# Iterated square roots of 1024 matrices, then a filtered Fourier layer: nine sets in flight instead of seven, and shorter rounds

## The chip, the cores and the metric

The kernel runs on one core of a Trainium2 chip. The metric is the device time of one execution in microseconds. Of the kernel before, three executions are shown: 3199.45, 3210.22 and 3218.83 us, median 3210.22. The profile is of one more execution, which took 3217.96 us.

[...] PE multiplies matrices into PSUM, DVE (VectorE) and ACT (ScalarE) read the results from there, POOL (GpSimd) adds what lies in SBUF, and SP issues most of the transfers; ACT issues those of the input.

## The reference, cut to what matters

`x` is 32 images of 32 channels of 128 x 128 float32. Two layers add to it:

```python
# layer 0, for each image and channel; gn normalizes groups of 2 channels
A = gn(x)
Y, Z = A / norm(A), I
for _ in range(5):
    T = 0.5 * (3.0 * I - Z @ Y)
    Y, Z = Y @ T, T @ Z
x = x + Y * sqrt(norm(A))
# layer 1
f = fft2(gn(x)).real
g = zeros; g[:32, :32] = einsum(f[:32, :32], weights1); g[-32:, :32] = einsum(f[-32:, :32], weights2)
x = x + ifft2(g).real
```

Layer 0 is 1024 independent chains of 128 x 128 products; layer 1 mixes the channels of an image, mode by mode.

## The kernel before, in words

**Sets.** Four channels of an image make a set; there are 256 sets, eight to an image. A set is a Python generator, `newton`, which yields after each step; the five iterations are folded there into two polynomials of fourth degree (`quartic`, called twice) and a last product. A step is nearly always: four products of 128 x 128 on PE into one bank of PSUM (`products`, L298, or `transposed`, L304), and one instruction of DVE (`plus`, L273) or ACT (`taken`, L267) that takes them out to SBUF. The next step needs that result. The chain of one set is v, w, q, then y, m, mb, again v, w, q, then t and y4, t, and the addition to xt at L410.

**Far and near.** w is a transposed v plus r. Images 1 to 19 (`is_far`) get it with transfers: DVE transposes blocks of 32 x 32 (L360), SP stores the tile in DRAM (L362), a later step loads it again with its blocks exchanged (one transfer at L373, or four at L370 in the second `quartic`), and POOL adds r (L376). The other images get it with a transposition on PE. So an image of the first kind makes fewer products, and needs more transfers.

**Rounds.** The loop at the end steps through lanes: each of the `LANES` lanes holds one set, and each round takes every lane one yield further. A new set enters a free lane when `due` allows: one per `FAR` rounds for a far image (20/7, since `newton` takes 20 steps and there are 7 lanes), one per `NEAR` rounds for a near one (13/4), which also needs fewer than `LESS` lanes taken. As a set enters, the normalization of the next is queued (`staged`), and the input of a later one is fetched (`fetch`, on ACT's queue). The tile scheduler then orders the instructions by the order of the program, their dependencies and its own estimate of when each is ready; instructions within `kept` stay in program order on their engine.

**Other generators** are stepped in the same loop: `prep` (statistics of the next image, from tiles `xs` loaded on ACT's queue, L193), `settle` (stores xt into `mid` at L418, folds it on POOL at L423, takes statistics at L427), `forward` and `spectrum` (the forward transform), `wide_products` and `small_products` (channel mixing, for a group of 21, then 8, then 3 images), and `inverse` (back transform, L742 to L781). Only after all sets of a group are there can its mixing begin, so inverses run beside the sets of the images from 20 on, and those of the last images after the last set.

**Buffers.** `rooms` gives, for each kind of tile, how many buffers of 128 x 512 float32 there are for the whole run, and how many more in the pool `early`, which is closed after the far images (`change`); `four` takes turns between the two. `far` decides there whether the second are used.

## Time and profile before

| | |
|---|---|
| profiled execution | 3217.96 us |
| its span | 3216.0 us |
| granted clock of TensorE, mean | 0.971 |
| PE busy | 2973.3 us (92%) |
| DVE busy | 2365.3 us (74%) |
| ACT busy | 1716.3 us (53%) |
| POOL busy | 2008.4 us (62%) |
| moved by DMA | 637.55 MB, mean 198 GB/s |

The page lists busy time by engine, by 40 slices of the span, and by line, each line with the idle time of its engine just before it and what ended that. A queue's name with a q (SPq) is the time of its sequencer, which issues transfers. In lists of waits, the line before the arrow waited for what stands after it; the numbers are microseconds in all, how often, and the longest. Four stages can be told apart: far images until about 1720 us, a passage until 1890, near images with mixing and inverses until about 2990, and the end.

### The profile page before, as it was taken

Reading aid. Unit: us, or ns where it says so; the run is one execution under the profiler, and the core shown is the slowest. Engines: PE = TensorE matmul, PEld = TensorE weight load, DVE = VectorE, ACT = ScalarE, POOL = GpSimd, SP = SyncE. Lnnn points to the kernel's source line nnn. Section 1 sums busy time; section 2 is a strip of 40 time slices with the busy share of each in tenths; the row PEclk is TensorE's granted clock in tenths of the full one; section 3 lists DMA queues with packets and bytes.
Section 4 is the critical chain, followed back from the end, with each engine's and each line's share of the span. In section 5 each row is a group of like instructions: output and inputs, shape, how many; then the busy total and the mean of one; then the engine's idle time right before and its main releaser. Section 6 shows DMA issues by size and latency. Waiting matters only on the chain.

```text
span 3216.0 us, 78946 instructions
## 1 busy us (share of the span) xinstructions
PE 2973.3 (92%) x29440; PEld 2836.6 (88%) x29440; DVE 2365.3 (74%) x5672; ACT 1716.3 (53%) x4148; POOL 2008.4 (62%) x2312
## 2 busy tenths in 40 slices
PE   6999999999999999999999999999999998999954
PEld 6889899899999999999999998898889888999853
DVE  5787788778888887888788665577767776756645
ACT  3555555565556655565565555455555544546533
POOL 3566666666767666666676553466767767746642
PEclk9999999999999999999999999999999999999975
DMA  3466566666666666666666336765767676576667
GB/s 122 148 190 190 192 201 202 186 199 204 196 208 200 210 191 196 207 204 200 191 211 193 96 96 207 227 214 185 232 201 243 213 240 208 193 225 209 207 238 255
DMA packets 482317, 637.55 MB, mean 198 GB/s; under 512 B 97936, under 2 KB 263056, under 8 KB 481936
## 3 DMA queue, kind: packets, MB, share of 16 engines
q1 hardware_dynamic: 366448, 413.30, 40.3%
q10 hardware_dynamic: 113472, 211.86, 21.1%
q0 software_dynamic: 2016, 7.34, 0.6%
q8 instruction: 235, 3.85, 0.5%
q14 instruction: 146, 1.20, 0.1%
HBM read 398.75 MB, written 233.57 MB: 197 GB/s over the span
## 4 chain that ended last, share of the span: by engine, by line
PE 67%; DVE 13%; DMA 12%; ACT 3%; issue 2%; POOL 1%; SPq 1%; ACTq 0%; DVEq 0%; POOLq 0%
PE ps L298 55%; PE ps L304 6%; DMA xs<-in_xt 5%; DMA turn<-turn 2%; PE ps L764 1%; DMA w<-turn 1%; DVE a_st L193 1%; PE ps L442 1%; DVE turn L360 1%; DVE q L273 1%; DVE yt L781 1%; DVE v L273 1%; PE ps L576 1%; PE ps L742 1%; DVE xt L410 1%
## 5 line engine op out<-in xcount | busy, mean ns | idle before, releaser
L298 PE MATMUL ps<-w,v 128*128 128x128 f32 x4096 | 548.5, 278 | 26.4 <-POOL w L376 14.1
L376 POOL TENSOR_TENSOR w<-w,r 128x512 f32<-128x512 f32 x304 | 386.7, 1275 | 270.5 <-DMA w<-turn 222.0
L298 PE MATMUL ps<-y,q 128*128 128x128 f32 x4096 | 549.6, 278 | 3.9 <-ACT y L267 2.2
L423 POOL TENSOR_TENSOR fold<-xt 128x256 f32<-128x256 f32 x512 | 363.7, 731 | 279.2 <-DVE xt L410 262.5
L328 ACT ACTIVATE b<-b,a_off,a_scr 128x128 f32<-128x128 f32 x1024 | 463.9, 489 | 129.7 <-issue 54.8
L298 PEld LDWEIGHTS ps<-w,v 128*128 128x128 f32 x4096 | 500.5, 193 | 35.2 <-POOL w L376 20.1
L298 PEld LDWEIGHTS ps<-y,q 128*128 128x128 f32 x4096 | 504.7, 194 | 7.0 <-ACT y L267 3.3
L273 DVE SCALAR_TENSOR_TENSOR q<-ps,eye 128x512 f32<-128x512 f32 x512 | 347.0, 678 | 99.5 <-PE ps L298 97.9
L717 POOL TENSOR_TENSOR yt<-yt,d 128x512 f32<-128x512 f32 x236 | 297.9, 1289 | 188.0 <-ACT d L776 155.0
L193 DVE BATCH_NORM_STATS2 a_st<-xs 128x6 f32<-128x128 f32 x1024 | 231.8, 279 | 143.4 <-DMA xs<-in_xt 143.0
L335 POOL TENSOR_SCALAR x<-xt,a_nm,a_sc 128x128 f32<-128x128 f32 x720 | 317.8, 454 | 23.9 <-DVE a_n L222 20.8
L404 ACT ACTIVATE y<-ps,a_t_s 128x128 f32<-128x128 f32 x1024 | 292.1, 369 | 62.3 <-PE ps L298 61.5
L292 POOL TENSOR_TENSOR r<-b,eye 128x512 f32<-128x512 f32 x104 | 132.8, 1277 | 283.8 <-issue 224.6
L298 PE MATMUL ps<-m,q 128*128 128x128 f32 x2048 | 280.3, 280 | 27.9 <-DVE q L273 27.6
L298 PE MATMUL ps<-m,mb 128*128 128x128 f32 x2048 | 282.4, 282 | 19.6 <-ACT mb L267 19.6
L273 DVE SCALAR_TENSOR_TENSOR v<-ps,x 128x512 f32<-128x512 f32 x256 | 175.5, 686 | 165.0 <-PE ps L298 162.9
L273 DVE SCALAR_TENSOR_TENSOR v<-ps,m 128x512 f32<-128x512 f32 x256 | 174.7, 683 | 162.8 <-PE ps L298 162.1
L298 PE MATMUL ps<-y,t 128*128 128x128 f32 x2048 | 280.6, 281 | 6.6 <-DVE t L273 4.5
L298 PEld LDWEIGHTS ps<-m,q 128*128 128x128 f32 x2048 | 252.1, 194 | 35.4 <-DVE q L273 17.9
L360 DVE STREAM_TRANSPOSE turn<-v 128x512 f32<-128x512 f32 x304 | 277.9, 914 | 7.2
L298 PE MATMUL ps<-x,b 128*128 128x128 f32 x2048 | 275.6, 278 | 5.6 <-POOL x L335 5.6
L298 PEld LDWEIGHTS ps<-m,mb 128*128 128x128 f32 x2048 | 254.9, 196 | 27.7 <-ACT mb L267 25.0
(124 smaller groups left out, 5867.6 us busy)
## 6 DMA issues: line engine op xcount, KB each, us to landing
turn<-turn SPq DMA_DIRECT2D x304, 256.0 KB
b<-in_x ACTq DMA_DIRECT2D x256, 256.0 KB
xt<-in_xt ACTq DMA_DIRECT2D x256, 256.0 KB
xs<-in_xt ACTq DMA_DIRECT2D x256, 256.0 KB
mid<-xt SPq DMA_DIRECT2D x256, 256.0 KB
yt<-mid SPq DMA_DIRECT2D x128, 512.0 KB
out<-yt SPq DMA_DIRECT2D x108, 512.0 KB
w<-turn SPq DMA_DIRECT2D x152, 256.0 KB
```

The source lines that it names most:

```text
L193: nc.vector.bn_stats(st[:, 4 * i + c, :], tiles[i][:, c, :])
L273: nc.vector.scalar_tensor_tensor(s, ps, f, t, ALU.mult, ALU.add)
L292: nc.gpsimd.tensor_tensor(r, mb, eye, ALU.add)
L298: nc.tensor.matmul(ps[:, j, :], lhsT[:, j], rhs[:, j], start=True, stop=True)
L304: nc.tensor.transpose(ps[:, j, :], t[:, j, :], ident)
L328: nc.scalar.activation(t, x, AF.Identity, bias=offset[:, c], scale=scale[:, c])
L335: nc.gpsimd.tensor_scalar(m[:, j, :], xt[:, j, :], nm[:, c // 2 : c // 2 + 1], sc[:, c : c + 1], ALU.add, ALU.mult,)
L360: nc.vector.transpose(blocks(t), v.rearrange(form, b=4))
L376: nc.gpsimd.tensor_tensor(w, w, r, ALU.add)
L404: nc.scalar.mul(y[:, j, :], py[:, j, :], sn[:, c : c + 1])
L423: nc.gpsimd.tensor_tensor(f[:, :, 64 * half : 64 * half + 64], xt[:, :, 0:64], xt[:, :, 64:128], op)
L717: engine.tensor_tensor(yh, yh, d, op)
```

## The change

- **Lanes and rounds.** `LANES, LESS` become 9 and 5, `FAR, NEAR` 27/9 and 25/5. Each step of a set yields twice (`rest`), but for the last. A far set takes 28 rounds instead of 20, a near one 24 instead of 13. The extra yields that only far sets had at q and t are gone. In far sets, one yield lay between store and load of a factor, and two between load and addition; now it is two and two, and the rounds are shorter in the near stage. A set's entry counts a far lane as 0.6 of a near one.
- **Buffers.** `rooms` is dealt anew, and whether a tile may lie in `early` is decided by `has_more`, which holds for the first 166 sets. `xs` has four buffers.
- **Statistics of a group.** `settle` takes the statistics of two channels, which are one group, in one instruction (L427): two of 256 elements for four of 128. `moments`, `avg_0` and `b_st` follow; the values computed are the same.
- **Other generators.** `step` goes on to the next generator of a queue when one is done. Mixing is stepped in two of three rounds, not in each; inverses in one of three, and in the round after the first half of a block (`holding`), where before it was four of five, or each one at the end.

```diff
-LANES, LESS = 7, 4
-FAR, NEAR = 20 / 7, 13 / 4
+LANES, LESS = 9, 5
+FAR, NEAR = 27 / 9, 25 / 5
...
+MORE = FIRST * 8 + 6
...
-    nc.vector.memset(avg_0, -P * P / 512)
+    nc.vector.memset(avg_0, -P * P / 256)
...
-    stp = ctx.enter_context(tc.tile_pool(name="stp", bufs=3))
+    stp = ctx.enter_context(tc.tile_pool(name="stp", bufs=4))
...
-        f = st.rearrange("p (g c) (e t) -> p g (c e) t", c=2, t=3)
+        per = st.shape[1] // G
+        f = st.rearrange("p (g c) (e t) -> p g (c e) t", c=per, t=3)
...
-        nc.vector.tensor_copy(nm, pm)
-        d = small.tile([P, G, 4], F32, tag=f"{tag}_d", name=f"{tag}_d")
+        nc.vector.tensor_scalar_mul(nm, pm, 2 / per)
+        d = small.tile([P, G, 2 * per], F32, tag=f"{tag}_d", name=f"{tag}_d")
...
-    rooms = dict(b=(6, 2), xt=(10, 5), x=(4, 3), r=(4, 3), v=(3, 3), w=(3, 3), q=(3, 3), y=(4, 3))
-    rooms.update(m=(3, 3), mb=(2, 1), t=(3, 2), y4=(2, 2), turn=(0, 3))
+    rooms = dict(b=(4, 2), xt=(10, 4), x=(3, 2), r=(5, 2), v=(3, 3), w=(3, 2), q=(4, 2), y=(4, 2))
+    rooms.update(m=(4, 2), mb=(2, 1), t=(3, 2), y4=(2, 2), turn=(0, 4))
...
+    def has_more(b, g):
+
+        return b * (C // 4) + g < MORE
...
             kept(nc.sync.dma_start(out=held, in_=t.rearrange("p c x -> p (c x)")))
-            yield
-            w = four("w", far)
+            yield from rest
+            w = four("w", more)
...
-            yield
-            yield
+            yield from rest
             nc.gpsimd.tensor_tensor(w, w, r, ALU.add)
             w = blocks(w).rearrange("p a c j -> p c a j")
         else:
-            yield
-            w = plus(transposed(v), 1.0, r, "w", far)
-        yield
-        q = plus(products(v, w), 1 / (16 * QS * QS), eye, "q", far)
-        yield
-        if far:
-            yield
+            yield from rest
+            w = plus(transposed(v), 1.0, r, "w", more)
+        yield from rest
+        q = plus(products(v, w), 1 / (16 * QS * QS), eye, "q", more)
+        yield from rest
         return q
 
-    def newton(g, sn, xt, m, mb, r, far):
+    rest = (None, None)
+
+    def newton(g, sn, xt, m, mb, r, far, more):
...
-        m = taken(products(q, y), "m", far, MS)
-        yield
-        mb = taken(transposed(m), "mb", far, QR * QS / MS)
-        r = plus_eye(mb, far)
-        yield
+        m = taken(products(q, y), "m", more, MS)
+        yield from rest
+        mb = taken(transposed(m), "mb", more, QR * QS / MS)
+        r = plus_eye(mb, far, more)
+        yield from rest
...
-        for j in range(4):
-            nc.vector.bn_stats(st[:, 4 * g + j, :], xt[:, j, :])
+        for j in range(2):
+            nc.vector.bn_stats(
+                st[:, 2 * g + j, :], xt[:, 2 * j : 2 * j + 2, :].rearrange("p c h -> p (c h)")
+            )
...
                 if not i:
+                    holding.append(b)
                     yield
+                    holding.pop()
...
-        if queue and next(queue[0], queue) is queue:
+        while queue and next(queue[0], queue) is queue:
             queue.pop(0)
...
-            room = lanes[i] is None and (far or LANES - lanes.count(None) < LESS)
-            if todo and room and rounds >= due:
+            under_way = [is_far(lane[0]) for lane in lanes if lane]
+            room = far or under_way.count(False) + 0.6 * under_way.count(True) < LESS
+            if lanes[i] is None and todo and room and rounds >= due:
...
-            if i == 0 or tail:
+            if i == 0 and rounds % 3 or tail:
                 step(prods)
-            if i == 0 and (rounds % 5 or len(ended) > B - 6) or tail and not (posts or specs):
+            if i == 0 and (rounds % 3 == 0 or holding) or tail and not (posts or specs):
                 step(backs)
```

## The prediction

> **What bounds the kernel now.** I read the busy shares of the page, then the same by stage (the far stage, the passage to the next, the near stage, the end), then PE's waits, a stretch of its timeline, and SP's queue.

> ```profile
> PE 2973.3 (92%) x29440; PEld 2836.6 (88%) x29440; DVE 2365.3 (74%) x5672; ACT 1716.3 (53%) x4148; POOL 2008.4 (62%) x2312
> ...
> 60.00:1720.00 1660.00, 1588.86 (x14047) 1531.84 (x14048) 1336.02 (x3209) 960.72 (x2368) 1105.20 (x1220) 0.99 0.63 195
> 1720.00:1890.00 170.00, 168.57 (x1523) 162.64 (x1522) 119.70 (x331) 87.36 (x208) 101.11 (x135) 1.00 0.38 120
> 1890.00:2990.00 1100.00, 1044.15 (x11438) 985.70 (x11437) 754.61 (x1803) 564.77 (x1345) 680.64 (x816) 0.99 0.65 211
> 2990.00:3216.00 226.00, 140.09 (x2234) 127.53 (x2233) 122.22 (x215) 87.57 (x193) 101.32 (x105) 0.75 0.72 236
> ```

> The columns are stretch, length, busy us of PE, PEld, DVE, ACT and POOL, clock, DMA share, GB/s. PE sets the time until 2990 us and is idle for 1660 - 1589 = 71 us in the far stage, 1.4 us in the passage and 1100 - 1044 = 56 us in the near stage. Busy time hides a little more. The densest pieces of the chain show the floor:

> ```profile
> 599.87 9.83 PE ps L298 x88
> ```

> 88 PE instructions in 9.83 us are 0.1117 us each; I call that a slot. A product of four matrices is eight slots, 0.89 us. The far stage's 14047 instructions at that rate take 1569 us, so 91 us of its 1660 are excess: the 71 idle, and 20 at a lower clock or in short hiccups. The passage runs at 170/1523 = 0.1116 us: with nothing late, this code reaches the floor. So the most that can be won before 2990 us is about 91 + 56 + 11 (1% of clock in the near stage) = 158 us.

> Which waits make the idle time? PE's own, in the far stage (first four lines) and in the near stage (three lines):

> ```profile
> PE ps L298 <- ACT mb L267: 19.6, 21, 3.4
> PE ps L298 <- POOL w L376: 14.1, 17, 2.1
> PE ps L304 <- ACT m L267: 11.5, 8, 4.2
> ...
> PE ps L298 <- ACT t L267: 3.0, 2, 2.3
> ...
> PE ps L298 <- DVE q L273: 22.3, 16, 6.0
> PE ps L304 <- DVE v L273: 8.7, 3, 6.4
> PE ps L298 <- DVE w L273: 8.6, 7, 2.9
> ```

> (total us, times, longest.) Four kinds make 48 of the 71 us, three make 40 of the 56. All are steps of one set that follow each other too closely on PE. The timeline shows one:

> ```profile
> 1001.94 0.63 PE L304 MATMUL ps<-ident,m 128*128 128x128 f32 x4
> 1003.32 1.16 PE L298 MATMUL ps<-m,mb 128*128 128x128 f32 x8 [0.75 <-ACT mb L267]
> ```

> The product that needs mb is the next thing on PE after the transposition that yields it; ACT's copy (598 ns in its row) lies open between them. SP's queue shows the same of the loads of factors:

> ```profile
> SPq L373 <- DMA turn<-turn: 198.1, 104, 5.4
> SPq L370 <- DMA turn<-turn: 175.9, 105, 4.2
> ```

> 209 loads stood at the head of SP until the store that they read back had landed, 1.8 us each; stores behind them waited too, and so did POOL (222.0 us in 125 waits for w<-turn).

> [...] products recorded at 1.06 us each start 0.89 us apart, so I use starts. [...] Here the longest waits are 3.4 to 6.4 us and the clock is 0.99 in both long stages, so at most 1% lies there. [...] DVE stood at statistics L193 for DMA xs (143.0 us, longest 7.3) while evacuations lay behind. [...]

> **The change part by part.** Its work on PE is the same, 29440 instructions. What changes is the order. I counted, in the order of PE's instructions in the two built programs, how many slots lie between a product and the one that needs its result (medians), and turned them into time with 0.1117 us.

> *Nine lanes, two rounds a step, far stage.* A round stays about as long: 20/7 = 2.86 rounds a set become 28 rounds over 9 lanes = 3.11. A step was one round, now two. Distances: y,q to transposition of m 18 to 48 slots (2.0 to 5.4 us); that to m,mb 24 to 56 (2.7 to 6.3; some were 0); t 32 to 52 (3.6 to 5.8). The gain of 2.2 to 3.6 us exceeds nearly every wait there (longest 3.4, 4.2, 2.3; means 0.9, 1.4, 1.5). Of 19.6 + 11.5 + 3.0 = 34.1 us I count 90% as gone: 31. The distance before y<-q hardly moves (48 to 56 for x,q, the same for m,q), but it costs only 2.6 us there: 0.

> *Loads of factors.* The load (one DMA, or four of 64 KB; 152 + 608 in all) goes from 24 to 48 slots after its store, 2.7 to 5.4 us, past at most one more store on SP. That covers SP's 1.8 us, so it is issued without standing; the addition on POOL stays 22 slots behind it, and the product that uses w goes from 52 to 74 slots behind that. Store to use: 120 to 172 slots, 13.4 to 19.2 us. POOL's wait for the DMA was 1.8 us on average: it mostly goes, and PE's 14.1 us with it. I take 12. Behind POOL's addition stand r, x and fold, which come earlier then.

> Clock in the far stage: 1% of 1660 is 17 us; with fewer pauses half returns, 8. Far stage in all: 31 + 12 + 8 = 51 us. The other 23 us of idle time (statistics L204, L504 and such) keep their distances: 0.

> *Five near lanes of 24 rounds, one set per 5 rounds.* Distances: v to its transposition 24 to 50 slots, w 32 to 46, q 28 to 44: 1.6 to 2.9 us more. Mean waits were 2.9, 1.2 and 1.4, but the longest 6.4, and these come from DVE standing at xs, which stays. I take 60% of 22.3 + 8.7 + 8.6 + 3.9 (m, mb and t) = 26 us, and half of the clock's 11: 5. Near stage 31 us.

> *Statistics over two channels.* 512 calls of 256 elements for 1024 of 128. A call occupies DVE for 236.5/1024 = 0.231 us; per element, the 512-wide sums against the 128-wide call give (0.68 - 0.28)/384 = 1.05 ns, so a wide call is about 0.365 us. 1024 x 0.231 - 512 x 0.365 = 50 us less DVE work, all hidden: DVE is busy 80% in the far stage and 69% in the near, behind PE. On the path 0; between 0 and 10 if DVE's queue matters. Without cover it would be the 50.

> *Pools.* Seventy-seven tiles of four matrices instead of 83, for more sets. I looked how long each buffer stands free, from its last reader to its next writer, in the built order: xt at least 112 slots (12.5 us; it was 286), v 70, w 86, y 72, x 64 in the far stage, b 67 in the near one; x in the near stage down to 0, but is filled long before use. Cost 0, and the slower rival below if a landing outlasts the gap. The fourth xs buffer moves the load from 24 to 30 slots ahead of its statistics in the far stage and not at all in the near (30, 29): 0.

> *Pace of products and inverses.* Two rounds of three and one of three (with the second half of an inverse right after its first). In order, inverse 0 starts 176 slots earlier, inverse 27 38 earlier, and what follows the last set is the same, inverses 28 to 31. The end costs the same 226 us. The short hold of PSUM banks could help PE's weight loads that waited for ACT d (18.3 us in the near stage); peak use of banks is unchanged, so 0, up to 10.

> *Sum.* 51 + 31 = 82 us. The profiled execution took 3217.96 us, its span 3216.0: 3134 of span, 3136. The median of the runs shown, 3210.22, lies 8 us below the profiled one: **3128 us**, 2.6% faster.

> **Rivals.**
> 1. *More comes back.* Half-clock stretches, banks and hiccups follow the pauses: 75 of 91 us far, 50 of 67 near, 3085. For it: the passage at 0.1116 us; against: statistics L204 and xs are untouched. Chance 0.14.
> 2. *The waits move.* DVE's standing at xs, up to 7.3 us, is longer than the new 5 to 6 us, and the q distances stay short; only POOL's and ACT's far waits shrink by half, 22 us: about 3190, between 3165 and 3225. For it: 72 of the 143 us of xs fall in the near stage. Chance 0.16.
> 3. *Slower: ACT stands at a fetch.* xt is fetched on ACT's queue; its 14 buffers serve nine lanes, those staged and those settling. If the store into mid lands later than 12.5 us after the last reader's place, ACT blocks with all its copies behind. ACT idles (1660 - 961)/154 sets = 4.5 us a set; beyond that each us counts. At 5.2 us late: 154 x 0.7 = 108, far gain gone, near 31 kept, + 77: 3287. Against it: SP loses its standing at loads. Chance 0.12.

> **How the numbers follow.** Forecast 0.58, its own range 3100 to 3165. A change below 0.5% (16 us) can't be told from none. Faster: 0.58 + 0.14 + half of rival 2 = 0.80; the same 0.07; slower 0.12 + 0.01 = 0.13. Range 3080 to 3212: it leaves out rival 3 and the tips of 1 and 2.

> **What would show it.** PE's far waits for mb, m and w below 10 us together; SP's standing at L373 and L370's loads below 100 us; POOL's wait for w<-turn below 100; near waits for q, v, w near 16; stage times of about 1609 and 1069 us; wide statistics near 0.41 us each. Wrong would be: ACT waiting for DMA mid<-xt ahead of xt (rival 3), or PE's waits for q and v as large as before with xs ahead on DVE (rival 2).

## The result: 0.24% faster, a tenth of what was forecast

The changed kernel took 3199.91 us (median of 20 runs, 3189.05 to 3210.8), the one before 3207.38 (20 runs): a ratio of 0.9976, with a 95% interval of 0.9964 to 0.9989. Forecast were 3128 us, range 3080 to 3212, against 3210 before: a gain of 82 us. It was 7.5. The result lies inside the range, which was wide enough for the rivals, but outside the 3100 to 3165 us that the forecast gave itself. The profiled execution has a span of 3205.1 us against 3216.0.

The page and the windows of the changed kernel, with the same columns as before:

```profile
PE 2973.7 (93%) x29440; PEld 2850.6 (89%) x29440; DVE 2316.5 (72%) x5158; ACT 1701.5 (53%) x4148; POOL 2003.6 (63%) x2314
```

```profile
60.00:1720.00 1660.00, 1605.95 (x14232) 1558.02 (x14232) 1304.12 (x2935) 970.36 (x2396) 1117.20 (x1243) 0.98 0.64 198
...
1890.00:2990.00 1100.00, 1033.77 (x11303) 978.40 (x11302) 740.32 (x1618) 546.80 (x1324) 680.32 (x817) 0.98 0.65 213
```

In the far stage PE idles 54 us instead of 71, but its clock fell from 0.99 to 0.98; in the near stage it idles 66 instead of 56, and the clock fell as much. PE's waits show what took the place of the old ones, first in the far stage. Source lines have moved by two or more: L206 is the former L204, L509 the former L504, L300 the former L298, L447 the former L442.

```profile
PE ps L206 <- DVE a_qs L201: 16.0, 9, 2.6
PE ps L509 <- DVE b_qr L504: 8.1, 4, 2.7
PE ps L206 <- DVE b_r_q L150: 7.1, 2, 3.7
PE ps L206 <- DVE b_inv L521: 5.2, 2, 3.2
PE ps L206 <- DVE b_r_q L152: 4.4, 2, 2.5
PE ps L300 <- POOL w L381: 3.6, 2, 2.2
PE ps L306 <- ACT sw L464: 2.7, 8, 0.5
```

And in the near stage:

```profile
PE ps L206 <- DVE a_qs L201: 17.9, 6, 8.9
PE ps L447 <- POOL fold L426: 12.0, 6, 4.4
PE ps L300 <- ACT d L782: 11.3, 4, 4.5
PE ps L509 <- DVE b_qr L504: 6.7, 3, 3.1
```

The far waits for mb and t, 22.6 us together before, are gone from the list; that for m is 1.0 us, that for w 3.6 instead of 14.1. In the near stage q, v and w cost 39.6 us before and do not stand among the first now. In their place come two tiny products: L206, which averages an image's statistics across the partitions (two instructions of 32 columns), and L509, which does so for a spectrum. L206 reads only a_qs of what DVE makes; where the list names b_r_q or b_inv there, another instruction of DVE ended nearest to the release. Before, the wait for a_qs was short, in the far stage (first line) and in the near one:

```profile
PE ps L204 <- DVE a_qs L199: 6.9, 6, 2.1
...
PE ps L204 <- DVE a_qs L199: 3.2, 4, 1.1
```

One such place of the changed kernel on PE's timeline:

```profile
885.63 0.22 PE L512 MATMUL ps<-avg,b_mr 128*32 128x1 f32 x2
889.23 0.60 PE L206 MATMUL ps<-a_qs,avg_mean 128*128 128x32 f32 x2 [3.38 <-DVE b_r_q L150]
889.64 2.05 PE L300 MATMUL ps<-x,q 128*128 128x128 f32 x8
891.49 0.85 PE L300 MATMUL ps<-q,t 128*128 128x128 f32 x3
```

PE stands 3.4 us at L206 with ready products behind it. DVE meanwhile works through the chain that leads to a_qs, in which other instructions lie:

```profile
887.26 0.67 DVE L174 TENSOR_TENSOR a_d<-a_d 128x64 f32<-128x64 f32 x1
887.85 0.14 DVE L516 TENSOR_SCALAR b_v<-ps 128x1 f32<-128x1 f32 x1
887.92 0.14 DVE L517 COPY b_v<-ps 32x1 f32<-32x1 f32 x1
887.98 0.64 DVE L175 SCALAR_TENSOR_TENSOR a_d<-a_d,a_st 128x64 f32<-128x64 f32 x1
888.55 0.41 DVE L430 BATCH_NORM_STATS2 b_st<-xt 128x6 f32<-128x256 f32 x1
888.88 0.20 DVE L201 TENSOR_REDUCE a_qs<-a_d 128x32 f32<-128x64 f32 x1
```

And the next eight instructions of PE take 2.05 us instead of 1.06; the clock that the trace records is 0.50 from 887.74 to 894.57 us. Such stretches, recorded at 0.5, are called half clock here. Of the 14 in the far stage, 13 begin within 2 us of the end of a pause at L206 or L509. A pause, here and below, is the time between two starts on PE less one slot, and is counted where it exceeds 0.35 us. By stages, which end at the additions to xt that end images 0, 19 and 31 (all in us):

| | start | far | near | end | pauses far, near | half clock far, near |
|---|---|---|---|---|---|---|
| before | 135.4 | 1648.2 | 1309.4 | 123.1 | 80.9, 75.3 | 37.5, 41.0 |
| changed | 143.8 | 1631.2 | 1306.3 | 123.8 | 56.0, 83.1 | 58.0, 61.4 |

### The profile page after: what moved, and what is told of

Its sections match the earlier page's. It is cut to its first block, busy times and chain, and to the rows that moved or that the text cites. A ratio compares the mean times of both kernels' runs of the same rounds, so it can differ in the third digit from the quotient of the medians.

```text
span 3205.1 us, 78907 instructions
## 1 busy us (share of the span) xinstructions
PE 2973.7 (93%) x29440; PEld 2850.6 (89%) x29440; DVE 2316.5 (72%) x5158; ACT 1701.5 (53%) x4148; POOL 2003.6 (63%) x2314
## 4 chain that ended last, share of the span: by engine, by line
PE 68%; DVE 12%; DMA 11%; issue 3%; POOL 3%; ACT 2%; SPq 1%; ACTq 0%; DVEq 0%; POOLq 0%
PE ps L300 55%; PE ps L306 6%; DMA xs<-in_xt 4%; DMA w<-turn 2%; DVE turn L366 2%; PE ps L770 2%; PE ps L447 1%; DVE v L275 1%; DVE a_st L195 1%; POOL yt L723 1%; DVE q L275 1%; DMA yt<-mid 1%; PE ps L748 1%; DVE yt L787 1%; PE ps L581 1%
## 5 line engine op out<-in xcount | busy, mean ns | idle before, releaser
L300 PE MATMUL ps<-w,v 128*128 128x128 f32 x4096 | 556.2, 280 | 8.9 <-POOL w L381 3.6
L300 PE MATMUL ps<-y,q 128*128 128x128 f32 x4096 | 531.2, 278 | 11.8 <-ACT d L782 9.9
L300 PEld LDWEIGHTS ps<-w,v 128*128 128x128 f32 x4096 | 506.2, 195 | 13.3 <-POOL w L381 5.8
L300 PEld LDWEIGHTS ps<-y,q 128*128 128x128 f32 x4096 | 496.6, 195 | 16.0 <-ACT d L782 10.4
L195 DVE BATCH_NORM_STATS2 a_st<-xs 128x6 f32<-128x128 f32 x1024 | 227.2, 279 | 134.3 <-DMA xs<-in_xt 133.7
L294 POOL TENSOR_TENSOR r<-mb,eye 128x512 f32<-128x512 f32 x104 | 132.5, 1274 | 304.4 <-ACT mb L269 298.9
L300 PE MATMUL ps<-x,b 128*128 128x128 f32 x2048 | 279.4, 280 | 5.7 <-POOL x L341 5.6
L269 ACT ACTIVATE t<-ps 128x512 f32<-128x512 f32 x256 | 152.5, 596 | 247.6 <-PE ps L300 240.6
L300 PE MATMUL ps<-m,q 128*128 128x128 f32 x2048 | 280.1, 281 | 0.5 <-DVE q L275 0.5
L300 PE MATMUL ps<-m,mb 128*128 128x128 f32 x2048 | 280.2, 281 | 0.1
L300 PE MATMUL ps<-y,t 128*128 128x128 f32 x2048 | 277.4, 279 | 2.7 <-ACT d L782 1.4
L300 PE MATMUL ps<-x,q 128*128 128x128 f32 x2048 | 277.8, 279 | 1.9 <-DVE q L275 1.9
L413 DVE TENSOR_TENSOR xt<-ps,xt 128x512 f32<-128x512 f32 x256 | 175.4, 685 | 143.6 <-PE ps L300 141.0
L300 PE MATMUL ps<-q,t 128*128 128x128 f32 x2048 | 275.6, 278 | 0.0
```

Of the source, the lines that this page charges most:

```text
L195: nc.vector.bn_stats(st[:, 4 * i + c, :], tiles[i][:, c, :])
L300: nc.tensor.matmul(ps[:, j, :], lhsT[:, j], rhs[:, j], start=True, stop=True)
L413: nc.vector.tensor_tensor(xt, products(t, y), xt, ALU.add)
```

## The experiments

Each kernel was timed beside the kernel before, on the same chip; ratios are to that one.

**The statistics products three and two yields later, in the changed kernel.** The theory after the result: the waits were handed on to these products.

```diff
             q, d.rearrange("p g (c e) -> p (g c) e", e=2), AX.X, ALU.add
         )
-        yield
+        for _ in range(4):
+            yield
...
         nc.vector.tensor_copy(mr, ms[:, None, :].to_broadcast([P, 2, G]))
-        yield
+        for _ in range(3):
+            yield
```

> The changed kernel, with three more yields ahead of the product of an image's statistics (L206) and two more ahead of the product that sums a spectrum's statistics (L509). In the built order the first then stands about 90 slots behind the DVE instruction that it needs, instead of 2. Theory (the waits that the nine lanes removed were taken over by the statistics products, which stand too close on PE, and each such pause of 2 to 3 us is followed by a half-clock stretch): PE's waits at L206 and L509 fall from 78 us to under 10, the clock of the far stage goes from 0.98 to 0.99 or more, about 69 us of pauses and 20 of clock come back: 3110 us, at most 3140. Rival (DVE and POOL cannot supply more, so PE will wait for something else): 3185 to 3200 us, with new waits of the same sum.

Measured: 3119.15 us, ratio 0.9717 (0.9693 to 0.974), 9 us above the theory's figure and within its bound. The far stage fell from 1631.2 to 1572.0 us, the near one from 1306.3 to 1277.3. PE's waits in the far stage begin now with these (the source lines move by one more):

```profile
PE ps L307 <- ACT sw L465: 9.5, 15, 1.7
PE ps L301 <- POOL w L382: 6.4, 5, 2.2
```

The window of the far stage, with the columns as before:

```profile
60.00:1720.00 1660.00, 1639.38 (x14784) 1592.52 (x14786) 1359.58 (x3035) 1001.91 (x2470) 1152.90 (x1289) 1.00 0.66 202
```

PE idles 21 us there, at clock 1.00. The sum closes: far pauses fell from 56.0 to 22.0 us, 34 us; time at half clock from 58.0 to 3.4, half of which, 27 us, is counted as lost; together 61, measured 59. So, by this estimate, 27 of the 61 us that the two small products cost in the far stage were paid in clock, not in waiting. DVE and POOL have supplied the faster PE, with 1359.6 and 1152.9 us of work in that window instead of 1304.1 and 1117.2: the rival falls.

**The same yields in the kernel before.** The diff is the same.

> The kernel before, with the same yields. Theory: before, these products cost 18 us of pauses (10 and 4 at L204, 4 at L504) and perhaps 8 of clock, and the close steps of a set remain: 3180 us, between 3170 and 3200. If the statistics products were the only trouble in both kernels, it would come down as far as the changed one does, to about 3110.

Measured: 3221.22 us, ratio 1.0044 (1.003 to 1.0059); both expectations missed. The far stage gained 17.5 us, the near one lost 13.6. PE's far waits:

```profile
PE ps L299 <- POOL w L377: 23.9, 28, 2.3
PE ps L299 <- ACT mb L268: 17.4, 21, 4.2
```

The wait for w rose from 14.1 to 23.9 us, so that all far pauses fell only from 80.9 to 70.9 us, while those of the near stage rose from 75.3 to 84.9. Without the nine lanes much of the removed wait is handed back to the steps of a set. The whole change alone brings 0.24%, the later statistics alone cost 0.4%; together they bring 2.8%.

**The lanes alone.** The kernel before with lanes, yields, `rooms`, `has_more` and the entry rule of the changed one.

```diff
-LANES, LESS = 7, 4
-FAR, NEAR = 20 / 7, 13 / 4
+LANES, LESS = 9, 5
+FAR, NEAR = 27 / 9, 25 / 5
...
-        yield
+        yield from rest
```

> The kernel before with the lanes, the two rounds a step, the dealing of the buffers and the rule for entry of the changed one, and nothing else of the change (statistics of one channel, three xs buffers, pace of mixing and inverses and one generator a step as before). Theory: L204 stands 2 slots behind what it needs here too, so the lanes alone bring no more than the whole change: 3190 to 3205 us. Rival (the lanes brought their 80 us, and the other parts lost them again): 3125 to 3145.

Measured: 3235.1 us, ratio 1.0082 (1.006 to 1.0104). The theory's range was missed on the slow side, the rival by more. The far stage, 1614.6 us, is shorter than in the changed kernel. The statistics have moved to the front of its pauses already: 26.9 us at L205, where L204 had 9.6 before. The near stage takes 1360.8 us, 51 longer than before. There the rounds are shorter, and mixing and inverses, stepped by the round as before, go faster with them: the first addition of image 20's inverse comes at 2553 us instead of 2777. PE's pauses in the near stage are 116.0 us, with waits spread over statistics (16.1 at L205), sw, mb and the loads for mixing.

**The rest of the change without the lanes.**

> The changed kernel with lanes, yields, buffers and entry rule of before, the rest as changed. Theory: the other parts are worth little, within 10 us of before: 3197 to 3217. Rival (the other parts cost what the lanes won): 3260 to 3290.

Its diff is the one above turned round. Measured: 3294.73 us, ratio 1.0263 (1.0227 to 1.0298), just above the rival's range. Its near stage is short, 1224.2 us, since inverses are late (its far stage, 1682.2 us, is 34 longer than before); its end takes 259.1 us instead of 123.1. With long rounds, one step of an inverse in three of them is too slow: the first addition of image 20's inverse comes at 3114 us, after the last set. The end at clock 0.53:

```profile
3108.00:3295.00 187.00, 81.69 (x956) 69.84 (x944) 122.94 (x153) 65.80 (x137) 68.92 (x49) 0.53 0.90 310
```

So the loss is not one that the lanes made good in the changed kernel: the pace fits their short rounds and does not fit the long ones.

**Lanes and pace together, without the statistics of two channels and the fourth xs buffer.**

```diff
-            if i == 0 or tail:
+            if i == 0 and rounds % 3 or tail:
                 step(prods)
-            if i == 0 and (rounds % 5 or len(ended) > B - 6) or tail and not (posts or specs):
+            if i == 0 and (rounds % 3 == 0 or holding) or tail and not (posts or specs):
                 step(backs)
```

> The kernel before with lanes, yields, buffers and entry rule, and the pace of mixing and inverses with the holding rule and the next generator in the same step: the whole change but for the statistics of two channels and the fourth xs buffer. Theory (statistics of two channels and the fourth buffer are worth nothing; the pace takes back the near stage that the lanes alone lost to the short rounds): 3190 to 3210 us, near stage 1300 to 1315 us. Rival (the wide statistics are what kept the changed kernel from being slower): 3220 to 3240.

Measured: 3223.79 us, ratio 1.0041 (1.0027 to 1.0055), a little above the theory's range and inside the rival's. The near stage is 1306.5 us, as expected: the pace gives back what the short rounds took. The wide statistics and the fourth buffer then account for the rest to 0.9976, some 20 us by the two ratios; which of the two did it was not separated. (The two profiled spans differ by only 8.5 us, but this kernel's profiled execution was one of its fastest and the changed kernel's one of its slower ones.) The far stage, 1638.7 us, is 24 us longer than with the lanes alone. Of what was added, only the rule in `step`, the next generator in the same step, acts before mixing begins at 1907 us. It is therefore the likely cost, and would be a loss within the change itself, but it was not tested alone.

**Four instructions for the statistics of a set again, with the statistics products later.** There are three xs buffers here.

```diff
-        for j in range(2):
-            nc.vector.bn_stats(
-                st[:, 2 * g + j, :], xt[:, 2 * j : 2 * j + 2, :].rearrange("p c h -> p (c h)")
-            )
+        for j in range(4):
+            nc.vector.bn_stats(st[:, 4 * g + j, :], xt[:, j, :])
```

> The statistics products later, but the statistics of settle in four calls of 128 elements as before, for which one of the four xs buffers had to go (three, as before). Theory: 50 us of DVE's work are hidden behind PE: 3117 to 3130 us. Rival (DVE, 72% busy, is close enough to PE that its work counts): 3140 to 3170.

Measured: 3117.0 us, ratio 0.9712 (0.9689 to 0.9735), the same as with two. The instruction on 128 elements and that on 256, first in the list of groups of this kernel, then in that of the changed one (busy us, mean ns of one, idle time before):

```profile
L431 DVE BATCH_NORM_STATS2 b_st<-xt 128x6 f32<-128x128 f32 x1024 | 250.8, 280 | 6.0
```

```profile
L430 DVE BATCH_NORM_STATS2 b_st<-xt 128x6 f32<-128x256 f32 x512 | 207.5, 418 | 5.5
```

So the additional DVE work and the missing buffer show no cost where the statistics products stand far enough away, while together they cost some 20 us where PE stands at these products, as the run before showed.

**Only the image's statistics later.**

> The changed kernel with only the product of the image's statistics (L206) three yields later, not that of the spectrum (L509). Theory (each of the two pauses on its own, with its half clock): 55 of the 71 us of pauses go, 16 stay with some half clock: 3125 to 3145 us. Rival (one of them hides behind the other, so that moving one moves the wait to the other): 3160 to 3195, with L509's wait well above 16 us.

Measured: 3150.08 us, ratio 0.9813 (0.9792 to 0.9833), between the two expectations. The far stage has all of the gain (1576.4 us), the near one none (1307.9). Its first waits over both stages:

```profile
PE ps L301 <- ACT d L783: 19.0, 7, 4.1
PE ps L510 <- DVE b_qr L505: 13.2, 6, 4.0
PE ps L448 <- POOL fold L427: 12.7, 5, 4.4
```

L510 did not grow; the wait for ACT's copies d out of PSUM did (11.3 us in the near stage of the changed kernel). There, moving one of the two products alone brought nothing.

**One yield more instead of three and two.** How much distance is enough?

> The changed kernel with one more yield ahead of each of the two statistics products (instead of three and two more). The built order then has the first about 26 slots, 2.9 us, behind its DVE instruction instead of 2 or 90. Theory (the wait is as long as DVE's chain runs late, 2 to 4 us at most times): the far stage gains nearly all, the near one, with its shorter rounds, about half: 3125 to 3150 us. Rival (any slack is enough): 3115 to 3122; (only a long one is): 3165 to 3190.

Measured: 3122.6 us, ratio 0.9726 (0.9703 to 0.975), just below the theory's range and at the other's edge. Some 26 slots, 2.9 us, do nearly all, and the mean clock of the profiled execution is 0.977 instead of 0.965. PE's wait for a_qs is 8.3 us over both stages here.

**The loads of xs four ahead, with the statistics products later.**

```diff
-        for i in range(3):
+        for i in range(4):
             load(i)
...
-            if i + 3 < C // 4:
-                load(i + 3)
+            if i + 4 < C // 4:
+                load(i + 4)
```

> The statistics products later, and the loads of xs four ahead of their statistics instead of three (there are four buffers). DVE's standing at L195 for DMA xs was 129 us in 82 times, up to 6.6. Theory: with the products of a set two rounds apart this standing is covered: within 8 us of 3119. Rival (PE's remaining waits come from DVE standing at xs): DVE's wait falls below 60 us and the time to 3090 to 3105.

Measured: 3135.52 us, ratio 0.9778 (0.975 to 0.9805): some 16 us slower than with three, which neither expected. DVE's standing at xs hardly fell, from 128.6 to 115.5 us, and PE's waits for ACT's m and mb came back (9.9 and 5.9 us). The author's explanation is that, with all four buffers asked for at once, a load stood on ACT's queue until one was free, and copies behind it. ACT's waits that end with a landing of xs, such as this one, fit that, but it was not shown.

```profile
ACT b L335 <- DMA xs<-in_xt: 12.7, 4, 5.8
```

**The forward transform later too.** What was left after the first experiment were waits for fold and sw.

```diff
     def forward(b, q, u):
+        yield
...
         nc.scalar.copy(sw, ps)
         yield
+        yield
```

> The changed kernel with the statistics products later, as in the run of them alone, and the forward transform later too: one yield more between the folds on POOL and the products that read them, and one more between ACT's copy sw and its transposition. Theory (a pause on PE costs itself and a half-clock stretch): the waits for fold and sw that were left, 15 and 11 us with some 10 us of half clock, go: 3095 to 3108 us against 3119 without. Rival (nothing is left in the order, and the rest of the near stage is set by mixing and inverses): 3113 to 3125.

Measured: 3106.25 us, ratio 0.9676 (0.9652 to 0.97), inside the theory's range: 3.2% faster than before, and the best version here. The far stage takes 1562.2 us, the near one 1269.2. Its far waits have shrunk to four:

```profile
PE ps L301 <- POOL w L382: 8.8, 6, 4.2
PE ps L301 <- DVE xt L414: 2.9, 1, 2.9
PE ps L167 <- DVE a_ms L164: 0.7, 1, 0.7
PE ps L301 <- DVE t L276: 0.5, 1, 0.5
```

## Why the prediction was wrong

- **The failed step** is one sentence on the far stage: "The other 23 us of idle time (statistics L204, L504 and such) keep their distances: 0." The distances between the steps of a set had been counted in the built order; these were not. Counted now, the DVE instruction that makes a_qs stood about 15 slots (median) ahead of its product before, and stands 2 ahead in the changed kernel. Pauses at L204, 13.5 us over both stages, became 54.7 at L206; those at L504, 3.7 us, became 16.0 at L509. Moving the two products away, and nothing else, gave 3119 us, 9 below the forecast. The near stage was then 32 us shorter than before, where 31 had been counted, and the far one 76, where 51 had been: the 12 us of pauses that it had at L204 and L504 went too, and 17 us of clock came back instead of 8.
- **The near stage** made the same omission, and it took forward's products with it. With the next generator in the same step and shorter rounds, they come sooner after the folds: from 1780 to 3140 us PE waited 13.4 us for folds, and 5.2 with the lanes alone, without that rule. In the best version 3.6 us of such waits are left.
- **The clock** was counted at 8 + 5 us of gain, an estimate of the author's, and "at most 1%". It moved against that: half-clock time rose by some 20 us in each stage, although PE idled less in the far one. In these two traces it rose with the number of longer pauses, not with the sum of all: pauses of 2 us or more went from 8 to 15 in the far stage and from 12 to 15 in the near one, while all pauses of the far stage fell from 80.9 to 56.0 us.
- **The lanes and the loads of factors** did to PE what was worked out: m, mb, t from 34.1 us to 1.0, w from 14.1 to 3.6 in the far stage, q, v, w in the near one. SP's standing at turn<-turn fell from 374 to 68 us at its loads. But POOL's wait for w<-turn rose, from 222 to 301 us, where below 100 was foretold: the loads did not come late for PE, whose wait for w is 3.6 us, so it was off PE's path. That POOL simply came to them earlier was not shown.
- **The statistics of two channels**: 0.418 us each against 0.41 estimated. "0; between 0 and 10 if DVE's queue matters" was right in the kernels with distance, and low in the changed one, where they and a buffer together gave some 20.
- **The pools** show no cost, as counted: with the statistics later the same pools carry 3119 us. Larger pools were not tried.
- **The rivals.** Rival 2 foretold that the waits move, about 3190, and that was right in kind; but it put them at DVE's standing for xs in front of q and v, and these waits went. The place was wrong, and that its 3190 us lies near the 3200 measured is luck. Rivals 1 and 3 did not happen.

## What to carry to other kernels

When a change spreads out the steps of a pipeline, count the distances of everything on the bound engine, the tiny side jobs most of all: here a product of two short instructions held back the ready products behind it for 3.4 us. Such gaps came with a cost in clock as well: 34 us of pauses and, by estimate, 27 of clock in the far stage. And what is stepped once per round changes its pace when the length of a round changes, so the two are tuned together or not at all.

## What the runs showed of the hardware

What follows is counted in the profiles of two runs, the changed kernel and the one before. It tells what stood beside what in them, not why.

```profile
447.00:457.00 10.00, 7.33 (x43) 7.11 (x42) 6.28 (x16) 4.59 (x12) 6.24 (x7) 0.69 0.64 199
...
541.00:551.00 10.00, 7.85 (x55) 7.66 (x55) 8.95 (x26) 5.05 (x16) 6.12 (x8) 0.83 0.52 176
```

The DVE instructions on a_d, of 128 x 64 elements, took quite different times in the changed kernel. In the chain above two of them took 0.67 and 0.64 us, as long as the sums over 128 x 512 (0.68). There are 96. None of the 34 that ran while POOL stood idle took more than 0.25 us; 33 took more than 0.4, and each of these ended 80 to 106 ns after the end of an instruction of POOL. The reduction to a_qs never took more than 0.22 us, and the addition to xt took 0.63 to 0.72 with POOL busy or idle. The longest case was 6.87 us, at 2506.08: POOL worked without a pause from 2502.41 to 2512.87, and PE stood 8.9 us at L206 behind it. That DVE stood for POOL there, and that part of the wait for a_qs comes from it, is how the author reads these times; no run here takes POOL's work away, so neither that nor the size of such a part was shown.
